# Opening of an attention and MLP kernel: second half of the first batch beside the first-pass steps, and constant products on TensorE

## The chip, the cores and the metric

The kernel runs on one core of one Trainium2 chip. Times are device microseconds (us) of one execution. A profiled execution has a span, from its first to its last instruction, and its own time, which also holds what lies around the span.

## The reference

The input is x of 4 batches x 1024 tokens x 256 channels. Two sandwich layers follow.

```python
x = x + layernorm(attention(layernorm(x)))
x = x + layernorm(ffn(layernorm(x)))
```

Attention has 16 heads of 16 channels. Its weights are binarized: each of Wq, Wk, Wv, Wp is replaced by its sign times the mean of its magnitudes, and each product adds a bias. Scores are scaled by 1/4 and go through softmax. The MLP has ternary weights: `silu(x w1 s1) * (x w2 s2)`, then two hidden layers of 1024 with exact gelu, then a product back to 256 channels.

## The kernel before

**What TensorE multiplies.** Products are done in fp32r, one pass. To keep fp32 accuracy a value is split into a high and a low fp32r piece, and both are multiplied; weights that are signs or ternary need no low piece. Where a product has plain fp32 operands (the means L249, L996, L1003, the bias L405, the last projection L1407), the trace shows two rows for each instruction.

**The opening** (from L193, before the branch) is one list of instructions for each engine. x of batch 0 comes in two halves of 512 tokens. VectorE (DVE) measures the first half (`measure_half(0)`: `bn_stats` and `bn_aggr` on four tiles, then `rstd` on GpSimd, POOL). ScalarE (ACT) takes magnitudes and signs of the four weights. TensorE (PE) sums the magnitudes of Wq and Wk into `al` (L249) and the flag `fl` (L259), from which every engine later decides a branch: the fast path if no weight is over 2 (L1441). DVE normalizes the first half (`xn_first`), measures the second half (`measure_half(1)`), TensorE transposes the first half (L284), and ACT and DVE write the high and low pieces (L286, L287).

**The attention** starts behind the branch, again in an order written out by the program. Work is counted in steps. A block is one group of 4 heads and 512 queries and has 8 steps; there are 4 batches x 4 groups x 2 = 32 blocks. The first pass (L722) multiplies queries by keys, and DVE takes the maximum of each 128x512 tile (L731): four tiles in each step. The second pass (L768) multiplies keys by queries with the maxima subtracted by a third product, ACT takes the exponential (L778), and `attend` (L794) multiplies it by the values. The first pass runs ahead: it starts at step `first` = -10, the second pass at step 0. So in the ten steps from -10 to -1 TensorE has first-pass products and jobs, and no second pass.

`slots(s)` gives the products of step s in five parts, and jobs are put in two places of a step: `run_jobs(s, 0)` after the third part, `run_jobs(s, 1)` after the last. `place((s, slot), job)` chooses the place. Tiles of `through` (seven PSUM banks) are chosen by `bank()` from planned times of PE, ACT and DVE; each engine works off its list in order.

Ahead of step -10 TensorE has in the fast path: the two `first_heads` jobs for the first half of queries and keys (L566; ACT scales and adds the bias twice, L572 and L579, and DVE makes the low piece of q or the mixed piece of k, L584 and L587), and the two `turn` jobs (L477) that transpose the second half, which DVE has normalized (`norm(1, nc.vector)`, L465). The jobs in the ten steps are: `first_heads` for the second half, four `value` jobs (L494), four parts of the next group's queries and keys (L535, whose pieces POOL splits, L548 and L549), the two means `alphas` (L996, L1003), `projection_bias` (L405) and the transposition of the maxima (`shift`, L748).

**The MLP** (`mlp`) works on 8 blocks of 512 tokens. `gated` makes h; `hidden` twice makes g1 and g2 with eight chunks of 128 hidden channels each; `done(c)` of a chunk runs gelu on ACT (L1261), the split on DVE (L1188, L1189), and then whatever jobs `beside` holds for that chunk. In block 0 these are `norm` and `turn` of block 1 and the last eighth of attention's projection: `scale_y` (L1394) and `last_projection` (L1407, L1412, L1413), which multiplies, adds the bias, and normalizes into x.

Of the kernel before, what the change touches and what calls it, by code (L numbers as in the profile page):

```python
# [40 lines left out]
P = 128  # L41
# [5 lines left out]
def sandwich_kernel(  # L47
# [157 lines left out]
    with ExitStack() as octx:  # L205
# [17 lines left out]
        nc.vector.tensor_scalar(turned, lower, -2.0, 1.0, ALU.mult, ALU.add)  # L223
        first_stats = []

        def measure_half(i):
            mv = moments(NT // 2, f"x0_{i}")
            for n in range(NT // 2):
                measure_one(mv, n, x_sb[:, 0, i * NT // 2 + n, :], f"x0_{i}")
            first_stats.append((mv, rstd(mv[:, :, 1], NT // 2, f"x0_{i}")))  # L230

        measure_half(0)
        most = small.tile([P, 4], F32, tag="most", name="most", bufs=1)
# [12 lines left out]
        for i, n in enumerate("qk"):  # L246
            for c in range(KC + 1):
                for k in range(KC):
                    nc.tensor.matmul(  # L249
                        al[:, c, i : i + 1],  # L250
                        mag_of[n][:, k, bass.ts(c, P)] if c < KC else mag4[n][:, k, :],
                        avg[:, 0:1], start=(k == 0), stop=(k == KC - 1),
                    )
# [5 lines left out]
        nc.tensor.matmul(fl, large, row_ones, start=True, stop=True)  # L259

# [19 lines left out]
        measure_half(1)  # L280
        tr = [ps_p.tile([P, 512], F32, tag=f"tr{k}", name=f"tr_first_{k}") for k in range(KC)]
        for k in range(KC):
            for i in range(NT // 2):
                nc.tensor.transpose(tr[k][:, bass.ts(i, P)], xn[:, i, bass.ts(k, P)], ident)  # L284
            hi, lo = (f[:, k, 0:512] for f in (xnT_sb, w1_sb))
            nc.scalar.copy(hi, tr[k])  # L286
            nc.vector.tensor_sub(lo, tr[k], hi.bitcast(F32))  # L287


    def attention(signs):  # L290


        with ExitStack() as actx:
# [267 lines left out]
            def first_heads(is_q, j):  # L561

                t = bank()
                for k in range(KC):
# [14 lines left out]
                got([t], "ACT", nc.scalar.activation(  # L579
                    full, through[:, t, :], AF.Identity, bias=bias4[:, n : n + 1],  # L580
                    scale=alpha4[:, n : n + 1],
                ))
# [402 lines left out]

            def run_jobs(s, slot):
                for job in jobs.pop((s, slot), ()):
                    job()

# [20 lines left out]
            if signs:  # L1010
                quadrants(0)
                norm(1, nc.vector)
                for is_q in (True, False):
                    first_heads(is_q, 0)
                for k in range(KC):
                    turn(1, k)

                place((first, 1), lambda: first_heads(False, 1))
                place((first + 1, 1), lambda: first_heads(True, 1))
                for i, n in enumerate("vp"):  # L1020
                    place((first + 6 + i, 0), lambda n=n: alphas(n))
                after = first + 2
            else:
                part = group_jobs(0)
                norm(0, nc.vector)
                for k in range(KC):
                    turn(0, k)
# [86 lines left out]
    def mlp(tag, low_too, wp):  # L1114
        with ExitStack() as fctx:
# [283 lines left out]
            def last_projection():  # L1399
# [3 lines left out]
                for m in range(2):  # L1403
                    zp = ps_o.tile([P, 512], F32, tag="o", name=f"zp{tag}_{m}")
                    for i in range(2):
                        for k in range(KC):
# [3 lines left out]
                            )  # L1410
                        z = zs[2 * m + i]
# [12 lines left out]
            for blk in range(blocks):  # L1424
# [4 lines left out]
                if blk == 0:  # L1429
                    beside[6] = [scale_y]  # L1430
                    beside2[5] = [last_projection]
# [66 lines left out]
```

## Time and profile before

| | |
|---|---|
| time, median of 3 runs | 1568.97 us (1566.95 to 1570.28) |
| profiled execution, own time | 1567.72 us |
| its span | 1565.9 us |
| busy in the span: PE, DVE, ACT, POOL | 98%, 69%, 53%, 28% |
| mean granted TensorE clock | 0.993 |
| first L722 product, first L768 product | 23.29 us, 55.48 us |
| last projection's products (L1407) | 970.35 to 976.6 us |

Busy time is what the rows of an engine cover. Rows of TensorE are pipelined and their ends are modelled, so that a busy TensorE is not at its peak; the time from one row's start to the next says more. In timeline rows the columns are start, time covered, engine, line, operation, tiles, shapes, and the number of instructions; in brackets stands the idle time before and what ended it. In a view by stretches each engine's busy time and number of rows is given, then the granted clock as a share of full speed, the DMA share and GB/s.

### The profile page before, as it was taken

To read this page: it belongs to the slowest core of one execution; us is meant where nothing else is said; L and a number is where in the kernel's file an instruction comes from. 1 tells how busy PE (TensorE), PEld (TensorE's weight loads), DVE (VectorE), ACT (ScalarE), POOL (GpSimd) and SP (SyncE) were. 2 spreads that over 40 slices of the span, in tenths; PEclk is the share of its full clock that TensorE was granted. 3 is DMA by queue.
4 is the path that set the end of the run, shared out by engine and by line. 5 is a ranking of instruction groups with operands and counts; after the bars stand their busy time and mean duration, and the time that the engine had idled before them with its cause. 6 is when DMAs were issued, how large, how long until landed. Compare 5 with 4: busy or idle time off the path is not lost.

```text
span 1565.9 us, 31822 instructions
## 1 busy us (share of the span) xinstructions
PE 1531.1 (98%) x12988; PEld 980.3 (63%) x12988; DVE 1075.2 (69%) x1960; ACT 829.2 (53%) x1496; POOL 437.4 (28%) x595
## 2 busy tenths in 40 slices
PE   7999999999999999999999999999999999999998
PEld 5544445444444444454444477888888888888887
DVE  6889887899787798878899554554545544455453
ACT  4577777677777677777777841413232313232321
POOL 2223143564424563314612150120202020202010
PEclk8999999999999999999999999999999999999999
DMA  1311521133132033311312040000000000000000
GB/s 58 72 30 33 144 49 29 24 72 74 39 76 59 22 65 72 66 30 31 75 36 73 8 139 0 1 14 1 14 1 14 1 14 1 14 1 14 1 14 17
DMA packets 35084, 58.55 MB, mean 37 GB/s; under 512 B 9968, under 2 KB 21488, under 8 KB 34928
## 3 DMA queue, kind: packets, MB, share of 16 engines
q1 hardware_dynamic: 29760, 43.57, 12.8%
q0 software_dynamic: 3792, 11.54, 2.3%
q8 instruction: 104, 1.70, 0.4%
q10 hardware_dynamic: 1376, 1.31, 0.2%
q14 instruction: 52, 0.43, 0.1%
HBM read 24.40 MB, written 4.19 MB: 18 GB/s over the span
## 4 chain that ended last, share of the span: by engine, by line
PE 85%; DVE 9%; ACT 4%; issue 1%; POOL 1%; DMA 1%; SPq 0%; DVEq 0%; ACTq 0%; POOLq 0%
PE g L1218 30%; PE y L794 14%; PE through L768 12%; PE through L722 10%; PE p L1218 7%; DVE nm L731 5%; PE fzp L1332 4%; PE through L535 2%; ACT e L778 2%; PE through L494 1%; PE through L748 1%; PE through L637 1%; ACT ys L809 1%; DVE bnstp_x L175 1%; DVE yt L835 1%
## 5 line engine op out<-in xcount | busy, mean ns | idle before, releaser
L731 DVE TENSOR_REDUCE nm<-through 128x1 f32<-128x512 f32 x1024 | 643.5, 680 | 115.6 <-PE through L722 59.3
L778 ACT ACTIVATE e<-through 128x512 f32<-128x512 f32 x1024 | 545.4, 603 | 160.7 <-PE through L768 141.7
L722 PE MATMUL through<-ks,qs 32*128 32x512 f32 x2048 | 462.2, 445 | 3.8 <-DVE nm L731 2.7
L768 PE MATMUL through<-qs,ks 32*128 32x512 f32 x2048 | 442.6, 434 | 11.1 <-ACT e L778 7.3
L768 PE MATMUL through<-nmT,ones_r 32*128 32x512 f32 x1024 | 348.7, 450 | 0.4 <-ACT nmT L755 0.4
L794 PE MATMUL y<-e,v 128*32 128x256 f32 x4096 | 323.0, 393 | 0.0
L722 PEld LDWEIGHTS through<-ks,qs 32*128 32x128 f32 x2048 | 215.7, 184 | 106.4 <-issue 82.5
L1218 PE MATMUL g<-g,h_sb 128*128 128x512 f32 x1024 | 235.7, 390 | 0.0
L768 PEld LDWEIGHTS through<-qs,ks 32*128 32x128 f32 x2048 | 201.8, 183 | 44.6 <-ACT e L778 20.5
L1218 PEld LDWEIGHTS g<-g,h_sb 128*128 128x128 f32 x1024 | 191.7, 188 | 39.5
L768 PEld LDWEIGHTS through<-nmT,ones_r 32*128 32x128 f32 x1024 | 137.6, 182 | 91.7 <-issue 88.7
L794 PEld LDWEIGHTS y<-e,v 128*32 128x32 f32 x4096 | 86.5, 108 | 170.8 <-issue 150.7
L1261 ACT ACTIVATE g2f<-g,sh_sb 128x512 f32<-128x512 f32 x64 | 44.1, 688 | 200.5 <-PE g L1218 180.8
L1261 ACT ACTIVATE g1f<-g,sh_sb 128x512 f32<-128x512 f32 x64 | 44.1, 689 | 170.1 <-PE g L1218 166.9
L164 POOL TENSOR_SCALAR ve_fz<-mvp_fz 128x4 f32<-128x4 f32 (+1 forms) x8 | 1.9, 232 | 468.5 <-DVE mvp_fz L176 468.5
L1218 PE MATMUL g<-h,h1b_sb 128*128 128x512 f32 x512 | 126.4, 389 | 0.0
L1218 PE MATMUL g<-h,h1a_sb 128*128 128x512 f32 x512 | 126.4, 389 | 0.0
L1188 DVE CAST g<-g2f 128x512 fp32r<-128x512 f32 x64 | 27.8, 434 | 142.0 <-ACT g2f L1261 142.0
L1218 PE MATMUL p<-xnT_sb,w_sb 128*128 128x512 f32 x512 | 117.7, 390 | 0.0
L1218 PEld LDWEIGHTS g<-h,h1a_sb 128*128 128x128 f32 x512 | 96.1, 188 | 19.9
L1218 PEld LDWEIGHTS g<-h,h1b_sb 128*128 128x128 f32 x512 | 96.1, 188 | 19.9
L1218 PEld LDWEIGHTS p<-xnT_sb,w_sb 128*128 128x128 f32 x512 | 95.6, 188 | 19.9 <-issue 0.4
(204 smaller groups left out, 1515.8 us busy)
## 6 DMA issues: line engine op xcount, KB each, us to landing
qs<-h1b_sb SPq DMA_DIRECT2D x240, 64.0 KB, 2.4
ks<-h1b_sb SPq DMA_DIRECT2D x120, 64.0 KB, 2.4
wraw<-in_dram SPq DMA_DIRECT2D x28, 256.0 KB, 2.7
h_sb<-in_dram POOLq DMA_DIRECT2D x4, 1024.0 KB, 8.5
yT<-yt SPq DMA_DIRECT2D x112, 32.0 KB, 2.0
out_dram<-x_sb SPq DMA_DIRECT2D x7, 512.0 KB, 2.8
x_sb<-in_dram SPq DMA_DIRECT2D x3, 1024.0 KB, 5.3
w_sb<-in_dram POOLq DMA_DIRECT2D x3, 1024.0 KB, 8.4
```

Source lines behind the costliest of these rows:

```text
L175: nc.vector.bn_stats(st, z)
L494: put(t, nc.tensor.matmul(through[:, t, bass.ts(i, C)], xnT_of[b][j][:, k, bass.ts(2 * m + i, P)], w_in["v"][:, k, :], start=(k == 0 and j ...
L535: put(t, nc.tensor.matmul(through[:, t, :], w_in[tag][:, k, bass.ts(c, P)], xnT_of[b][i][:, k, bass.ts(j, 512)], start=(k == 0 and i == 0) ...
L722: put(t, nc.tensor.matmul(through[:, t, :], q_of[u][n][rows, bass.ts(qt, P)], k_of[u][rows, bass.ts(j, 512)], start=(n == 0), stop=(n == 1),))
L731: got([t], "DVE", nc.vector.tensor_reduce(nm_of[blk][:, n4, j, g : g + 1], through[:, t, :], AX.X, ALU.max, negate=True))
L768: t, nc.tensor.matmul(through[:, t, :], lhs, rhs, start=(n == 0), stop=(n == 2)),
L778: exps.append(got([t], "ACT", nc.scalar.activation(e_of[s, g], through[:, t, :], AF.Exp)))
L794: nc.tensor.matmul(y_of[blk][32 * g : 32 * g + 32, cols], v_sb[n // 2][:, n % 2, :, :].rearrange("p h d -> p (h d)")[:, bass.ds((4 * g4 + ...
L1188: nc.vector.tensor_copy(hi, full)
L1218: nc.tensor.matmul(out[c], wk, src[j][:, k, :], start=(k == 0 and i == 0 and j == 0), stop=(k == n_k - 1 and i == len(ws) - 1 and j == 1),)
L1261: nc.scalar.activation(g, ps, AF.Gelu, scale=scale[:, c : c + 1])
L1332: nc.tensor.matmul(out_ps[i][:, :C], g2[j][:, k, bass.ts(i, P)], wk, start=(k == 0 and n == 0 and j == 0), stop=(k == NF - 1 and n == len( ...
```

## The change

1. Ahead of the branch 60 products of the constant `avg` with itself (plain fp32, 128x128, into a PSUM tile `hot` that nobody reads) are put into TensorE's list: 28 ahead of the means, 8 after each of the first two groups of means, 2 after each of the small ones, 8 after the flag, and 4 after the transposes. The means are reordered: the full ones of q and k, then the small ones.
2. Of the second half's four tiles DVE measures two before and two after the low pieces of the first half.
3. In the attention, for steps below 0, each `run_jobs` also issues 4 products of `ones_r` with itself (fp32r, 128x128), so 80 in all.
4. The second half is normalized on POOL instead of DVE, and its `turn` jobs move from before the first pass to slot 1 of the second step and slot 0 of the third. `first_heads` of the second half move from the first two steps to the fourth; `value` jobs start two steps later; the means `alphas` move to the sixth and eighth step.
5. In `first_heads` of the first half, the second scaling is made on DVE instead of ACT.
6. In the MLP's block 0, `scale_y` and `last_projection` move from chunk 6 of g1 and chunk 5 of g2 to chunks 0 and 2 of g1, `norm` of block 1 from chunk 2 to chunk 6 of g1; and all four products of a bank of `zp` come before DVE reads it.

```diff
+        hot = ps_p.tile([P, P], F32, tag="hot", name="hot")
+
+        def keep_going(n):
+            for _ in range(n):
+                nc.tensor.matmul(hot, avg, avg, start=True, stop=True)
+
...
-        def measure_half(i):
-            mv = moments(NT // 2, f"x0_{i}")
-            for n in range(NT // 2):
+        def measure_half(i, tiles=range(NT // 2)):
+            if 0 in tiles:
+                first_stats.append([moments(NT // 2, f"x0_{i}")])
+            mv = first_stats[i][0]
+            for n in tiles:
...
         measure_half(0)
+        keep_going(28)
...
+        for cs, behind in ((range(KC), 8), ([KC], 2)):
+            for i, n in enumerate("qk"):
+                for c in cs:
+                    for k in range(KC):
...
+                keep_going(behind)
...
         nc.tensor.matmul(fl, large, row_ones, start=True, stop=True)
+        keep_going(8)
...
-        measure_half(1)
+        measure_half(1, range(2))
...
             nc.vector.tensor_sub(lo, tr[k], hi.bitcast(F32))
+        keep_going(4)
+        measure_half(1, range(2, NT // 2))
...
-                got([t], "ACT", nc.scalar.activation(
-                    full, through[:, t, :], AF.Identity, bias=bias4[:, n : n + 1],
-                    scale=alpha4[:, n : n + 1],
-                ))
+                if j == 0:
+                    got([t], "DVE", nc.vector.tensor_scalar(
+                        full, through[:, t, :], alpha4[:, n : n + 1], bias4[:, n : n + 1],
+                        ALU.mult, ALU.add,
+                    ))
+                else:
...
+            hot = ps.tile([P, 512], F32, tag="y", name="hot")
+
             def run_jobs(s, slot):
                 for job in jobs.pop((s, slot), ()):
                     job()
+                if signs and s < 0:
+                    for _ in range(4):
+                        nc.tensor.matmul(hot[:, :P], ones_r, ones_r, start=True, stop=True)
...
-                norm(1, nc.vector)
+                norm(1, nc.gpsimd)
                 for is_q in (True, False):
                     first_heads(is_q, 0)
-                for k in range(KC):
-                    turn(1, k)
-
-                place((first, 1), lambda: first_heads(False, 1))
-                place((first + 1, 1), lambda: first_heads(True, 1))
+
+                place((first + 1, 1), lambda: turn(1, 0))
+                place((first + 2, 0), lambda: turn(1, 1))
+                place((first + 3, 0), lambda: first_heads(False, 1))
+                place((first + 3, 1), lambda: first_heads(True, 1))
                 for i, n in enumerate("vp"):
-                    place((first + 6 + i, 0), lambda n=n: alphas(n))
-                after = first + 2
+                    place((first + 5 + 2 * i, 1), lambda n=n: alphas(n))
+                after = first + 4
...
                                 wp[:, k, :].bitcast(F32), start=(k == 0), stop=(k == KC - 1),
                             )
+                    for i in range(2):
                         z = zs[2 * m + i]
...
                 if blk == 0:
-                    beside[6] = [scale_y]
-                    beside2[5] = [last_projection]
+                    beside = {0: [scale_y], 2: [last_projection], 6: beside[2]}
```

More of the change, by code (lines that the diff above doesn't have):

```diff
@@ L223, in sandwich_kernel @@
         nc.vector.tensor_scalar(turned, lower, -2.0, 1.0, ALU.mult, ALU.add)
+        hot = ps_p.tile([P, P], F32, tag="hot", name="hot")
+        def keep_going(n):
+            for _ in range(n):
+                nc.tensor.matmul(hot, avg, avg, start=True, stop=True)
         first_stats = []
-        def measure_half(i):
-            mv = moments(NT // 2, f"x0_{i}")
-            for n in range(NT // 2):
+        def measure_half(i, tiles=range(NT // 2)):
[3 more added lines that the diff above has]
+            for n in tiles:
                 measure_one(mv, n, x_sb[:, 0, i * NT // 2 + n, :], f"x0_{i}")
-            first_stats.append((mv, rstd(mv[:, :, 1], NT // 2, f"x0_{i}")))
+            if NT // 2 - 1 in tiles:
+                first_stats[i].append(rstd(mv[:, :, 1], NT // 2, f"x0_{i}"))
         measure_half(0)
+        keep_going(28)
         most = small.tile([P, 4], F32, tag="most", name="most", bufs=1)
@@ L245, in sandwich_kernel @@
         al = ps_p.tile([P, 3, 2], F32, tag="al", name="al")
-        for i, n in enumerate("qk"):
-            for c in range(KC + 1):
-                for k in range(KC):
[L249 to L253, printed above, removed]
+        for cs, behind in ((range(KC), 8), ([KC], 2)):
+            for i, n in enumerate("qk"):
+                for c in cs:
+                    for k in range(KC):
+                        nc.tensor.matmul(
+                            al[:, c, i : i + 1],
+                            mag_of[n][:, k, bass.ts(c, P)] if c < KC else mag4[n][:, k, :],
+                            avg[:, 0:1], start=(k == 0), stop=(k == KC - 1),
+                        )
+                keep_going(behind)
         large = small.tile([P, 1], F32, tag="largep", name="large", bufs=1)
@@ L578, in first_heads @@
                 n = 1 - is_q
-                got([t], "ACT", nc.scalar.activation(
-                    full, through[:, t, :], AF.Identity, bias=bias4[:, n : n + 1],
-                    scale=alpha4[:, n : n + 1],
-                ))
+                if j == 0:
[4 more added lines that the diff above has]
+                else:
+                    got([t], "ACT", nc.scalar.activation(
+                        full, through[:, t, :], AF.Identity, bias=bias4[:, n : n + 1],
+                        scale=alpha4[:, n : n + 1],
+                    ))
                 if is_q:
@@ L1011, in attention @@
                 quadrants(0)
-                norm(1, nc.vector)
+                norm(1, nc.gpsimd)
                 for is_q in (True, False):
                     first_heads(is_q, 0)
-                for k in range(KC):
-                    turn(1, k)
-                place((first, 1), lambda: first_heads(False, 1))
-                place((first + 1, 1), lambda: first_heads(True, 1))
+                place((first + 1, 1), lambda: turn(1, 0))
+                place((first + 2, 0), lambda: turn(1, 1))
+                place((first + 3, 0), lambda: first_heads(False, 1))
+                place((first + 3, 1), lambda: first_heads(True, 1))
                 for i, n in enumerate("vp"):
-                    place((first + 6 + i, 0), lambda n=n: alphas(n))
-                after = first + 2
+                    place((first + 5 + 2 * i, 1), lambda n=n: alphas(n))
+                after = first + 4
             else:
```

## The prediction

> **What bounds the kernel now.** I read the chain that ended last first: TensorE (PE) holds 85% of it, so a delay of TensorE anywhere in the opening passes through the attention loop to the end. The chain inside the first 56 us is carried by TensorE blocks:
>
> ```profile
> 9.69 3.57 PE al L249 x16
> 17.02 2.06 PE through L566 x4
> ...
> 29.48 1.68 PE through L494 x8
> ...
> 42.91 1.15 PE through L494 x8
> ```
>
> The same eight products of L494 take 1.68 us at 29.5 and 1.15 us at 42.9. The view by stretches says why:
>
> ```profile
> 24.49:29.84 5.35, 4.50 (x22) 2.55 (x23) 3.63 (x7) 3.11 (x4) 0.00 (x0) 1.00 0.00 2
> 29.84:40.08 10.24, 10.24 (x42) 6.99 (x41) 6.46 (x12) 1.95 (x3) 1.89 (x2) 0.50 0.01 2
> 40.08:55.48 15.40, 15.39 (x90) 9.12 (x90) 13.66 (x23) 5.00 (x9) 6.35 (x11) 1.00 0.05 9
> ```
>
> After the length the columns are PE, weight load, DVE, ACT, POOL, then the granted clock. It is 0.50 from 29.84 to 40.08. That is what the products in the ten steps are aimed at. Before 23 us the column reads 1.00, but the rows don't: eight 512-column products of L566 start 0.43 us apart from 17.02 to 20.57, and 0.24 apart at 24.5. So the front also runs at half rate.
>
> Is TensorE idle in the steps, so that added products are free? The timeline at full clock, where the time from one block's start to the next is what a block costs:
>
> ```profile
> 42.17 0.73 PE L722 MATMUL through<-ks,qs 32*128 32x512 f32 x3
> 42.84 0.39 PE L494 MATMUL through<-w_sb,xnT_sb 128*128 128x256 f32 x1
> ...
> 43.98 0.75 PE L722 MATMUL through<-ks,qs 32*128 32x512 f32 x8
> 44.66 1.05 PE L996 MATMUL through<-avg,yT_last 128*128 128x1 f32 x8
> 45.65 0.73 PE L722 MATMUL through<-ks,qs 32*128 32x512 f32 x5
> 46.31 0.50 PE L535 MATMUL through<-xnT_sb,w_sb 128*128 128x512 f32 x1
> ...
> 47.44 0.73 PE L722 MATMUL through<-ks,qs 32*128 32x512 f32 x3
> 48.10 1.13 PE L1003 MATMUL through<-yT_last,avg 128*128 128x256 f32 x4
> 49.16 1.26 PE L722 MATMUL through<-ks,qs 32*128 32x512 f32 x8
> ```
>
> A block of first-pass products costs 0.66 us whether it holds 3 or 5, and 0.68 with 8. L494 costs 1.15, L535 and L566 1.13, L996 0.99, L1003 and L405 1.06, four transposes (L748, 54.14 to 54.73) 0.59. The blocks stand end to end. DVE needs 4 x 0.60 = 2.4 us of maxima a step, TensorE about 3.4. TensorE is the bound there, clock or not.
>
> **Part by part.**
>
> *The first pass, before.* From 23.29 to 55.48 (the first L768) are 32.2 us. Blocks in order: 15 of L722 (10.0), two of L566 (2.3), four of L494 (4.6), four of L535 (4.5), L996, L1003, L405, L748 (3.7): 25.1 us at full clock. The rest is 4.4 lost to the half clock (the seven blocks from 29.41 to 40.38 took 11.0 and cost 6.6 at full clock) and 2.7 of waits.
>
> *The first pass, after.* Twenty groups of four products of ones_r come in, one in each half step; the first falls into idle time before the first pass, 19 lie inside. Each also cuts a run of eight first-pass products into two blocks: 19 blocks instead of 15 (12.5, and 0.35 for the last one). The jobs are the same (15.1), and two turns of 0.59 move in (1.2). No row shows a 128x128 fp32r product. Its weight load is 128 columns wide as in L996, whose eight rows start 0.114 apart; streaming 256 columns (L494) goes at 0.12. I take 4 x 0.112 plus the change of kind (L996 has about 0.1 over its rows): 0.57 a group, 10.8 in all. Bounds: 0.35 (the four stream at half of L494's rate and reload nothing) and 1.0 (0.22 each, what 128 columns in plain fp32 would take by L1003's rows): 6.7 to 19. Sum 39.9 us.
>
> To this come two waits. The second half's normalization goes to POOL: L465 takes 1.22 us there (24 rows) against about 0.4 on DVE, behind the 2.7 us of constants that POOL writes from 17.11 to 19.80. With the front below, its four tiles are ready at about 31.9; TensorE stands at the first turn from 30.0 on, and all first-pass blocks queue behind it: 1.5 us. The next L535 waits 0.4 for the low half of the second turn. So 41.8 instead of 32.2: +9.6. The 2.7 us of former waits go; DVE, with 36 maxima and 3 us of other work (24.5), fits under it.
>
> *The clock.* TensorE will have nothing from about 24 to 26.9 (last L566 product to first first-pass product) and little at the turn. In before a stretch of 3.4 us with PE busy for 0.75 of it (26.4 to 29.84, and again 733.0 to 736.4) was followed by half clock, for 10.2 us here and for 3.4 us there. So I expect the products not to prevent one drop around 27 to 30. A stretch costs at most 1.7 us; I take two, 3.4 (bounds 0 and, with the clock low for all the first pass, 39.9 x 4.4/6.6 = 27).
>
> The Trainium skill, "TensorE: Matmul & The Clock Gate", section on HAM oscillation, names idle gaps over about 3.4 us as what brings the half rate (its next section lets short idle times do so too, without a measure). Here it came with no idle gap over 1.2 us, so the trace does not bear the rule out; by it the 3.4 would drop out (1581.3). The same page, Back-to-back issue gap, gives about 81 ns for a sustained 128-column product; the nearest row has 112, and by the page the 19 groups would be an estimated 2.4 us cheaper. Neither changes the sign.
>
> *Ahead of the branch.* 56 products of avg stand before the first transpose. Each is plain fp32, two rows: at half rate 0.43 (L249: 12 rows in 2.70, 0.213 apart), at full rate 0.223 (L996's spacing; half of L1003's for the streaming). The front of before:
>
> ```profile
> 10.56 2.70 PE L249 MATMUL al<-avg,mag_k 128*128 128x1 f32 x12
> 13.19 0.19 PE L259 MATMUL fl<-row_ones,large 128*1 128x1 f32 x2
> 13.31 1.97 PE L284 MATMUL tr_first<-ident,xn_first 128*128 128x128 f32 x8
> 17.02 0.77 PE L566 MATMUL through<-xnT_sb,w_sb 128*128 128x512 f32 x1 [1.74 <-DVE w_sb L287]
> ```
>
> The clock rose at 23.0, 6.0 us after dense work began at 17.0, so I let it rise 6.0 us after 1.1: 14 products cold and 14 warm end at 10.2. The means (24 rows, 2.7), fl (0.1) and 28 more products (6.2) put the first transpose at 19.3 instead of 13.31. That is a queue on TensorE: everything behind waits. Then the warm clock gives back: transposes, copies and DVE's subtractions end at 21.95 (16.87 before), since only two of the four measures stand ahead of the subtractions; L566's blocks take half as long, and with `full` on DVE (0.62 behind ACT's 0.78) ks is ready at 26.85 instead of 23.24. +3.6 us (bounds +1.0, all warm, and +7).
>
> *The tail of attention's projection in the MLP.*
>
> ```profile
> 970.35 1.02 PE L1407 MATMUL zp<-wp_sb,yT_last 128*128 128x256 f32 x4
> 972.86 1.99 PE L1407 MATMUL zp<-wp_sb,yT_last 128*128 128x256 f32 x8 [1.49 <-DVE z L1412]
> 975.44 1.13 PE L1407 MATMUL zp<-wp_sb,yT_last 128*128 128x256 f32 x4 [0.59 <-DVE z L1412]
> ```
>
> TensorE waits for DVE's read of the half bank: 5.9 us for 16 rows that need 3.6. With all four products of a bank ahead of DVE both waits go, -2.2. In the new place TensorE arrives at 929.56, when chunk 2 is done; DVE has then chunk 0's split (until 929.95) and the scaling (2 x 0.48, L1394) before it: 1.3 us of a new wait. Net -0.9 (0 to -2.2). The normalization of block 1, now in chunk 6, has twenty us until its turn: nothing.
>
> **Sum.** +3.6 +9.6 +3.4 -0.9 = +15.7 on the span of 1565.9. The profiled run's own time is 1567.72, so 1583.4; the median is 1.25 above it: 1584.7.
>
> **Rivals.**
>
> *Cheap products* (1572 to 1577): groups at 0.35, no drop, warm from the start: +1.0 +9.6 -4.1 -2 gives +4.5. For it: nothing shows this product. Against: a load precedes every product in each row.
>
> *The clock stays low through the opening* (1590 to 1608): in before three stretches with PE busy at 1.00 did not raise it, and the new steps hold less streaming. The full 27 instead of 3.4 gives 1608. Against: at 517.9 and 736.4 it was back after one stretch.
>
> *Faster* (1565.5): the products find free slots, the clock holds, and the first pass runs at DVE's pace. First maximum at 27.95, 24.5 us of DVE: the first L768 at 52.9 instead of 55.5, and -0.9 later. It decides where a half step leaves TensorE 0.57 us of slack; in 42.17 to 49.16 I find none, and 49.16 to 50.35 (1.19 for a 0.68 block) is the only place where it waited for DVE. That the products fail to hold the clock at all is inside the second rival.
>
> **How the numbers follow.** About 0.2% (3.1 us) can be told from no change. The forecast, +8 to +21 (1577 to 1590), 0.60; cheap products 0.13; clock low 0.14; no change 0.04; faster 0.09. The range of 1572 to 1604 leaves out the last two and the end of the third. Slower 0.87.
>
> **What would show it.** Right: first transpose near 19, first pass beginning near 27, groups of four on the new line costing about 0.57 from start to start, the first L768 (its new line) near 69 to 72, a clock of 0.50 for some stretch between 26 and 36, TensorE waiting on POOL at the first turn, no wait inside zp but one before it. Wrong: the first second-pass product before 57, or groups whose removal of idle time shows as DVE without gaps in the ten steps.

## The result, and the profile after

The kernel after takes 1605.91 us (median of 4 runs, 1599.3 to 1608.15), the kernel before 1568.48 beside it (1566.95 to 1570.28). The ratio is 1.0248, with an interval of 1.0217 to 1.0279: slower by 37 us. The profiled execution took 1608.15 us with a span of 1606.3, against 1567.72 and 1565.9 before, so the two traces differ by 40.4 us. A run more than 1.5% above the fastest of its kernel counts as slow and stands outside the ratios given here; there is one, of 1600.88 us in experiment 2.

First the row of the page that gives the granted clock in 40 slices of 40 us, then the view by stretches, with the columns of before (time and rows of PE, weight load, DVE, ACT, POOL; granted clock; DMA):

```profile
PEclk8569999999999999999999999999999999999999
```

```profile
5.79:26.28 20.49, 17.52 (x146) 16.71 (x145) 12.04 (x33) 7.58 (x17) 7.96 (x28) 1.00 0.18 56
26.28:60.00 33.72, 33.08 (x118) 23.96 (x119) 16.12 (x25) 6.47 (x10) 9.36 (x10) 0.50 0.01 3
60.00:104.78 44.78, 44.53 (x204) 31.07 (x203) 19.08 (x31) 10.79 (x20) 5.79 (x9) 0.50 0.20 35
104.78:150.00 45.22, 44.89 (x528) 21.17 (x528) 36.35 (x60) 32.87 (x63) 9.31 (x15) 1.00 0.12 34
```

The front runs at full clock from 5.79 on, as it was meant to. Then the clock falls at 26.28 and stays at 0.50 for 78.5 us, through the whole first pass and into the second. In all that time TensorE is shown busy for 77.6 of 78.5 us. Busy did not bring the clock back.

The timeline (start, time covered, engine, line, tiles, shapes, number; in brackets the idle time before and what ended it) shows where it fell and what a block costs afterwards:

```profile
18.89 1.04 PE L298 MATMUL tr_first<-ident,xn_first 128*128 128x128 f32 x8
...
23.51 0.56 PE L1016 MATMUL hot<-ones_r 128*128 128x128 f32 x4
```

```profile
26.93 1.22 PE L744 MATMUL through<-ks,qs 32*128 32x512 f32 x5 [2.85 <-DVE ks L609]
28.08 1.11 PE L1016 MATMUL hot<-ones_r 128*128 128x128 f32 x4
29.12 1.22 PE L744 MATMUL through<-ks,qs 32*128 32x512 f32 x3
...
32.47 1.11 PE L493 MATMUL through<-ident,xn 128*128 128x128 f32 x4
...
40.22 0.95 PE L1016 MATMUL hot<-ones_r 128*128 128x128 f32 x4
41.09 1.22 PE L744 MATMUL through<-ks,qs 32*128 32x512 f32 x3
...
93.03 0.80 PE L790 MATMUL through<-qs,ks 32*128 32x512 f32 x2
...
100.88 1.94 PE L816 MATMUL y<-e,v 128*32 128x256 f32 x16
```

First transpose at 18.89, first pass at 26.93 after 2.85 us without a product. From then on blocks are slow: a first-pass block (L744) goes 1.15 us from start to start instead of 0.66, a group of four 0.87 (40.22 to 41.09, after a job) to 1.04 (28.08 to 29.12). The first second-pass product (L790) stands at 93.03; the corresponding L768 of before stood at 55.48. That is 37.6 of the 40.4 us, and all of it is there before step 0.

In the MLP the edit did its work. All 16 rows of the last projection follow each other, with one wait ahead of them:

```profile
972.27 3.72 PE L1435 MATMUL zp<-wp_sb,yT_last 128*128 128x256 f32 x16 [0.97 <-DVE yT_last L1422]
```

**Which share of the array is used.** PE's busy time does not tell why the clock stayed down, so I worked out another number from the rows. A dense row of 512 columns starts 0.427 us after the one before at half clock, and I take half of that at full clock; columns in proportion; a plain fp32 row counts twice where the profile shows it once (transposes and products of `avg`). Each product counts by the part of the 128x128 array it covers, so a first-pass product (32 rows) counts a quarter. Weight loads count nothing. The sum over a stretch of 3.413 us (the length of the single dips, and every change of the clock here falls on that grid), divided by the stretch, is the share. It is an estimate: whether a row's columns are counted from its start or spread over the row moves a share by up to 0.06. In the kernel before the clock fell after a stretch with a share of 0.34 (26.43 to 29.84), stayed low through 0.72 and 0.67 and came back after 0.82. In the kernel after it fell after 0.24 (22.86 to 26.28), and the stretches that followed in the first pass had 0.22 to 0.71, none more. The theory that the experiments are to test: **the clock goes by the streamed share, with two thresholds far apart; the new groups and the moved jobs hold the share in the gap between them, so one fall lasts to the end of the first pass.**

### The profile page after: what moved, and what is told of

It is laid out like the page before. It is cut to its first block, busy times and chain, and to the rows that moved or that the text cites. A ratio compares the mean times of both kernels' runs of the same rounds, so it can differ in the third digit from the quotient of the medians.

```text
span 1606.3 us, 32219 instructions
## 1 busy us (share of the span) xinstructions
PE 1578.6 (98%) x13188; PEld 1022.1 (64%) x13188; DVE 1074.2 (67%) x1958; ACT 828.0 (52%) x1494; POOL 442.6 (28%) x599
## 4 chain that ended last, share of the span: by engine, by line
PE 86%; DVE 8%; ACT 3%; issue 1%; POOL 1%; DMA 0%; SPq 0%; DVEq 0%; ACTq 0%; POOLq 0%
PE g L1246 29%; PE y L816 14%; PE through L790 12%; PE through L744 10%; PE p L1246 7%; DVE nm L753 5%; PE fzp L1360 4%; PE through L551 2%; ACT e L800 2%; PE through L510 1%; PE through L770 1%; PE hot L229 1%; PE hot L1016 1%; PE through L659 1%; ACT ys L831 1%
## 5 line engine op out<-in xcount | busy, mean ns | idle before, releaser
L744 PE MATMUL through<-ks,qs 32*128 32x512 f32 x2048 | 473.9, 456 | 5.6 <-DVE ks L609 2.9
L790 PE MATMUL through<-qs,ks 32*128 32x512 f32 x2048 | 445.2, 436 | 11.3 <-ACT e L800 7.6
L790 PE MATMUL through<-nmT,ones_r 32*128 32x512 f32 x1024 | 350.9, 453 | 0.4 <-ACT nmT L777 0.4
L744 PEld LDWEIGHTS through<-ks,qs 32*128 32x128 f32 x2048 | 220.7, 189 | 105.2 <-issue 80.2
L790 PEld LDWEIGHTS through<-qs,ks 32*128 32x128 f32 x2048 | 203.8, 184 | 44.7 <-ACT e L800 21.5
L790 PEld LDWEIGHTS through<-nmT,ones_r 32*128 32x128 f32 x1024 | 138.7, 183 | 92.2 <-issue 89.1
```

What stands on the lines that cost most here:

```text
L744: put(t, nc.tensor.matmul(through[:, t, :], q_of[u][n][rows, bass.ts(qt, P)], k_of[u][rows, bass.ts(j, 512)], start=(n == 0), stop=(n == 1),))
L790: t, nc.tensor.matmul(through[:, t, :], lhs, rhs, start=(n == 0), stop=(n == 2)),
```

## The experiments

Times here are medians beside runs of the kernel before on the same chip; the kernel after did not run beside them, so a difference from its 1605.91 us is good to a few us only. The runs of before scatter more than in the first comparison (1560.4 to 1574.4 over three sets), and so do some variants, because the stretches run on freely and a fall comes or not by where they lie. Over 48 runs of before, a line through time against time at half clock (twice one minus the mean granted clock, times the run's time) has 0.37 us lost per us at half clock, and 1559.0 at none; I use such lines below to take the clock out.

**1. The change without the groups of four.** Against the kernel after:

```diff
-                if signs and s < 0:
-                    for _ in range(4):
-                        nc.tensor.matmul(hot[:, :P], ones_r, ones_r, start=True, stop=True)
```

> The changed kernel without the 80 products of ones_r in the ten steps; all else stays, the 60 products of avg ahead of the branch too. Theory (the clock falls in the idle time before the first pass, 24.1 to 26.9 us, and comes back only after a stretch of 3.4 us in which the array is used for about three quarters; the groups of four small products hold TensorE for 0.87 us and use the array for 0.43 of it, so they keep the steps under that): the clock falls near 26 as in the changed kernel, but the steps are as dense as those of before, and it returns after 3 to 6 stretches; first second-pass product near 62, time 1573 to 1579. Rival A (the moved jobs make the steps thin, the products have no part in it): the clock stays at 0.50 until about 75 or later, time 1583 or more. Rival B (the clock is a side matter, the 80 products' own time on TensorE is the loss): about 1570, whatever the clock does.

Measured 1590.62 us (1589.07 to 1591.92), ratio 1.0169 (1.0136 to 1.0202). The clock is at 0.50 from 26.3 to 87.7. So the groups of four are not what keeps the clock down; my theory's number was missed and the first rival's held. The first pass with its jobs moved later (highest share of a stretch before the second pass 0.73) does not bring the clock back by itself either.

**2. The groups of four alone.** Against the kernel before: the same lines added to `run_jobs`.

> The kernel before with nothing added but the 80 products of ones_r in the ten steps. Theory: in before, the stretch from 26.4 to 29.8 uses the array for about a third and the clock falls after it; two groups add 0.12, so it holds or nearly holds. If it holds, the products cost their own time: 19 groups of 0.57 and four cut blocks, some 14 us, less the 4.4 of low clock: 1577 to 1581, first second-pass product near 65. If it falls all the same, it stays low for most of the first pass, as in the changed kernel: 1588 to 1600. Rival A (products of constants do not count for the clock at all): it falls at about 30 as in before and stays low: 1588 or more. Rival B (own time alone): 1582 with the same 10 us of low clock as in before.

Measured 1584.2 us (1569.39 to 1600.88, 10 runs), ratio 1.0087 (1.0053 to 1.012), on three levels: three runs at 1569.4 to 1570.8 with a mean clock of 0.998 or more, six at 1582 to 1586 with 0.986 to 0.988, one at 1600.9 with 0.975. The line through the nine runs of the first two levels has 0.39 us per us at half clock and 1568.3 at none. So the groups cost 9.3 us with the clock held (the expectation had some 14), and up to 17 more by the clock in these nine. In the profiled run (1585.48) the clock fell at 46.80. The stretches around it, and the rows:

```profile
22.91:43.39 20.48, 19.89 (x127) 14.65 (x127) 15.17 (x25) 6.86 (x10) 3.02 (x4) 1.00 0.01 1
43.39:46.80 3.41, 3.41 (x27) 2.54 (x26) 2.26 (x5) 0.59 (x1) 0.76 (x1) 1.00 0.23 38
46.80:80.93 34.13, 33.88 (x157) 23.12 (x156) 16.03 (x26) 8.48 (x16) 5.78 (x9) 0.50 0.22 40
```

```profile
43.35 0.56 PE L993 MATMUL hot<-ones_r 128*128 128x128 f32 x4
43.84 0.73 PE L722 MATMUL through<-ks,qs 32*128 32x512 f32 x5
44.51 0.66 PE L993 MATMUL hot<-ones_r 128*128 128x128 f32 x4
45.10 0.73 PE L722 MATMUL through<-ks,qs 32*128 32x512 f32 x3
45.76 1.05 PE L1001 MATMUL through<-avg,yT_last 128*128 128x1 f32 x8
46.67 1.00 PE L993 MATMUL hot<-ones_r 128*128 128x128 f32 x4
47.60 1.22 PE L722 MATMUL through<-ks,qs 32*128 32x512 f32 x5
```

This stretch is the plainest evidence of the whole case: in the stretch ahead of the fall TensorE is busy 3.41 of 3.41 us, the blocks stand end to end, and the clock falls. What fills the stretch is first-pass blocks on a quarter of the array, groups of four, and L1001 (the means `alphas`), eight rows of one column in 0.91 us. Its share is 0.26.

**3. A bridge over the idle time.** Against the kernel after:

```diff
                 if signs and s < 0:
-                    for _ in range(4):
+                    early = s < first + 3
+                    for _ in range(12 if (s, slot) == (first, 0) else 3 if early else 0):
+                        nc.tensor.matmul(hot, ones_r, xnT_sb[:, 0, 0:512], start=True, stop=True)
+                    for _ in range(0 if early else 4):
                         nc.tensor.matmul(hot[:, :P], ones_r, ones_r, start=True, stop=True)
```

> The changed kernel with the idle time before the first pass filled: twelve 512-column products of ones_r and the first high piece in the first slot of step -10, and three of them instead of the four small ones in each other half step up to step -8; from step -7 on the four small ones as in the changed kernel. Theory: TensorE's clock holds at full through the first pass, since it never has a stretch under a third; a group of four small ones costs about 0.57, first second-pass product at 68 to 73, time 1580 to 1586. Rival A (moved jobs or constant products cannot hold the clock): it falls once the wide products end, near 40, and the time is 1593 or more. Rival B: as the changed kernel, about 1605.

Measured 1576.56 us (1574.42 to 1591.59, 5 runs), ratio 1.0095 (1.0046 to 1.0144): three runs at 1574.4 to 1576.6 with a clock of 0.997 to 0.999, two at 1590.2 and 1591.6 with 0.986 and 0.987. The theory had 1580 to 1586. Filling the gap ahead of the first pass (27 wide products in place of 24 of the small ones) took away 29 us. In the profiled run the clock held until 51.24 and fell after the stretch with `alphas` in it (share 0.39), as in the run before.

**4. One wide product in place of each group of four.** Against the kernel after:

```diff
-                    for _ in range(4):
-                        nc.tensor.matmul(hot[:, :P], ones_r, ones_r, start=True, stop=True)
+                    nc.tensor.matmul(hot, ones_r, xnT_sb[:, 0, 0:512], start=True, stop=True)
```

> The changed kernel with each group of four 128-column products replaced by one 512-column product of ones_r and the first high piece: the same 512 columns streamed with one weight load. Theory: the clock falls near 26 as in the changed kernel, but a group now takes about 0.55 instead of 0.87 at half clock for the same use of the array, the steps reach three quarters, and the clock returns within 3 to 7 stretches (36 to 50 us); first second-pass product at 70 to 80, time 1580 to 1592. Rival A (these steps cannot raise the clock): low until the second pass has begun, about 1599. Rival B (own time alone): 19 x 0.3 less than the changed kernel, about 1600.

Measured 1579.05 us (1574.24 to 1580.02), ratio 1.0094 (1.0062 to 1.0126), a little under the expected range. The profiled run fell at 25.46 like the kernel after, but was back at 39.11, after a stretch with a share of 0.75 (the three stretches before it, of 0.32 to 0.68, had not brought it back). From start to start such a product costs 0.32 us after a job where the four cost 0.49. The wide product also streams x where the four stream ones; constant operands alone are not what fails, though: in the kernel after, the products of `avg` at the front brought the clock to full at 5.80.

**5. Wide or streaming nothing, at the same price in time.** Two variants of the kernel before whose groups take TensorE about as long as the four, with opposite shares. One has two products of `avg` with one column:

```diff
+                if signs and s < 0:
+                    for _ in range(2):
+                        nc.tensor.matmul(hot[:, :1], avg, avg[:, :1], start=True, stop=True)
```

> The kernel before with, in each half step of the first ten steps, two products of avg with a single column of avg (four rows, about 0.45 to 0.6 us of TensorE as a group of four costs, but next to nothing streamed) in place of the change's groups of four. Theory: what the clock goes by is how much of the array's time is streamed in a stretch of 3.4 us; these groups take the same time from TensorE and stream nothing, so the share falls below 0.35 early in the first pass and never comes to 0.75: half clock from about 27 to 33 until the y products of the first query group, the first second-pass product at 85 to 97, 1592 to 1612 in every run. Rival: the clock goes by TensorE's busy time, weight loads among it, and falls only in idle time: as with the groups of four alone, 1569 to 1586.

and the other two of 512 columns:

```diff
+                if signs and s < 0:
+                    for _ in range(2):
+                        nc.tensor.matmul(hot, ones_r, xnT_sb[:, 0, 0:512], start=True, stop=True)
```

> The kernel before with, in each half step of the first ten steps, two products of 512 columns (0.47 us at full clock, nearly all of it streamed) in place of the change's groups of four, which take 0.49 after a job. Theory: the same time from TensorE, but the share of the array in use stays above 0.4 in every stretch of the first pass, that with the products of alphas among them: the clock holds from 23 us on in all or nearly all runs, first second-pass product at 62 to 65, 1568 to 1572, and none of the spread to 1585 that the groups of four alone gave. Rival: the fall at the alphas comes from something else (a phase, chance): the same two levels, 1570 and 1585, about as often as with the groups of four alone.

One column: 1599.0 us (1598.24 to 1600.98, all five runs), ratio 1.0229 (1.0216 to 1.0242). 512 columns: 1572.5 us (1570.93 to 1584.13, 6 runs), ratio 1.0057 (1.0044 to 1.007); five runs at 1570.9 to 1574.8, one fell at 47.80 after the stretch with `alphas` (share 0.37). TensorE is shown busy almost without a break in both; the clock tells them apart. First the one-column variant's first pass by stretches, then the first pass of the 512-column one up to its fall:

```profile
25.28:59.42 34.14, 34.14 (x130) 26.04 (x129) 13.86 (x23) 7.00 (x10) 3.77 (x4) 0.50 0.03 5
```

```profile
20.50:44.39 23.89, 22.18 (x120) 13.95 (x118) 16.49 (x27) 9.50 (x15) 3.28 (x4) 1.00 0.00 1
44.39:47.80 3.41, 3.41 (x21) 2.00 (x20) 2.32 (x4) 0.57 (x2) 0.52 (x1) 1.00 0.23 38
```

In the first row PE is busy for 34.14 of 34.14 us at a clock of 0.50 throughout. Busy time, weight loads included, as what raises the clock is excluded by this row. For the wide pairs I had expected none of the spread to 1585; one run in six still fell.

**6. The front and the moved jobs.** First the kernel after without its front products (`keep_going` and its calls are taken out, which is all 60 products, the 4 after the first transposes among them), then without any constant product (also the lines of experiment 1):

> The kernel after without its 56 products of avg in the front; the groups of four in the ten steps, the moved jobs and the edit in the MLP stay. Theory: the front term (+3.6 us for the first pass) is real, and the clock falls in the idle time that the front leaves ahead of the first pass. Without the 56 products the first transpose stands near 13.3 again and ks is ready at 22 to 24 instead of 26.9; the clock rises near 23 as in the kernel before, and what follows depends on where the stretches of 3.4 us fall: 1570 where the clock holds, 1580 to 1600 where it falls. Rival: the groups of four and the moved jobs keep the clock down by themselves whatever the front does: 1598 to 1606 in every run, and half clock through the whole first pass.

> The kernel after without any of the constant products (neither the 56 in the front nor the groups of four): what is left is the moved jobs, the normalization on POOL, one subtraction pair of the measures later, and the edit in the MLP. Theory: at half clock L572 streams only 3.5 us without a break (15.48 to 19.0 in the run without the front products), as the turn's transposes no longer follow it, so hardly ever does a stretch of 3.4 us lie wholly inside; the clock does not rise there, and the rest of the first pass has no dense stretch either: ks at about 21.8, half clock until the first y products near 80, 1580 to 1590 in most runs, and 1558 to 1566 in a run where it does rise. Rival: without the groups the moved jobs are harmless, as dense as in the kernel before: 1558 to 1568 in all runs, half clock over by 24 to 40.

Without the front products: 1599.35 us (1598.17 to 1600.93), ratio 1.0224 (1.0211 to 1.0237), the rival's number. ks was ready at 21.8, so the front term is real (26.93 with them), but the time is hardly better. The rows:

```profile
16.48 0.63 PE L572 MATMUL through<-xnT_sb,w_sb 128*128 128x512 f32 x1
16.90 0.63 PE L572 MATMUL through<-w_sb 128*128 128x512 f32 x1
...
21.80 1.22 PE L734 MATMUL through<-ks,qs 32*128 32x512 f32 x5 [1.81 <-DVE ks L599]
```

512 columns go every 0.43 us, a first-pass block takes 1.15: the whole opening runs at half clock from the start. (The granted clock of this run reads 1.00 before 553 us and 0.997 in the mean; the record lacks the opening, and the rows decide.) In the kernel before these eight products were followed at once by eight transposes, 5.5 us without a break, and the clock rose at 23. The change moved the transposes into the first pass; what is left is 3.6 us of L572 and one group of four, and the best stretch there has a share of 0.68.

Without any constant product: 1582.86 us (1582.3 to 1583.24), ratio 1.0107 (1.0072 to 1.0142), as expected, with this detail against the expectation: in the profiled run the stretch from 15.51 to 18.92 did raise the clock (share 0.90), and the next, with 2.56 us of waiting for ks, took it away again until 73.5. So the moved jobs, even with the edit in the MLP, cost 15.5 us, although the first pass began at 21.48 instead of 23.29: the clock stood at 0.50 from 22.34 to 73.53.

**7. The edit in the MLP alone.** Against the kernel before:

```diff
-                    beside[6] = [scale_y]
-                    beside2[5] = [last_projection]
+                    beside = {0: [scale_y], 2: [last_projection], 6: beside[2]}
...
+                    for i in range(2):
                         z = zs[2 * m + i]
```

> The kernel before with only the edit in the MLP (all four products of a bank ahead of VectorE's reads, the scaling and the projection's tail in earlier chunks). Theory: -0.9 to -1.4 us on the span, both old waits inside zp gone and one new wait of about 1 us ahead of it: runs of 1559 to 1568, a median 1 to 2 below the kernel before. Rival: the waits only change place, no difference to 0.3 us.

Measured 1563.1 us (1559.26 to 1566.79, 12 runs), ratio 0.9987 (0.9973 to 1.0001). The sign is as expected; the interval includes no difference. The traces say more: from the 3585th of the 4096 `y` products to the end of the span are 750.8 us in before (1565.9 less 815.1) and 749.5 here (1560.2 less 810.7), 749.6 in the kernel after. The edit is worth 1.3 to 1.4 us.

**8. Out of the trap.** Against the kernel after, twenty wide products once, after the clock has fallen:

```diff
+                    for _ in range(20 if (s, slot) == (first + 1, 0) else 0):
+                        nc.tensor.matmul(hot, ones_r, xnT_sb[:, 0, 0:512], start=True, stop=True)
```

> The kernel after with twenty products of 512 columns added in the first half of the second step, after the clock has fallen. Theory: the half clock is a trap with one way out, a stretch of 3.4 us with the array nearly full; the twenty give two such stretches (8.5 us at half clock), the clock returns at 33 to 38 and then stays as long as no stretch falls below about 0.35: half clock for 7 to 12 us instead of 78, first second-pass product at 73 to 80 instead of 93, 1587 to 1594 although more work was added; up to 1604 where it falls again at the alphas. Rival: the clock is set by what the steps are, not by how they are entered (it falls again at once): 1610 to 1616.

Measured 1595.34 us (1593.89 to 1599.09), ratio 1.0195 (1.0159 to 1.0231): 10 us faster than the kernel after, with more work in it. That is a little over the 1587 to 1594 of the theory, and within its second case, up to 1604 where the clock falls again at the alphas. The view by stretches shows both:

```profile
22.95:26.36 3.41, 1.14 (x8) 0.88 (x6) 2.46 (x4) 1.56 (x2) 3.38 (x13) 1.00 0.00 0
26.36:33.19 6.83, 6.21 (x19) 4.21 (x20) 3.14 (x5) 0.00 (x0) 5.57 (x6) 0.50 0.00 0
33.19:53.67 20.48, 19.98 (x123) 15.12 (x121) 12.51 (x20) 6.57 (x10) 3.32 (x4) 1.00 0.01 1
53.67:57.08 3.41, 3.41 (x25) 2.54 (x25) 1.87 (x3) 0.61 (x2) 0.47 (x1) 1.00 0.22 38
57.08:91.22 34.14, 33.89 (x147) 24.85 (x145) 15.46 (x26) 8.41 (x15) 5.79 (x9) 0.50 0.19 34
```

Idle time takes the clock (share 0.22). The dense stretch from 29.78 to 33.19 (0.82) gives it back. The steps keep it for 24 us. The busy stretch with `alphas` (0.28) takes it again, and the steps, the same in kind, do not get it back for 34 us. The rival, that the clock falls again at once, is excluded by the 24 us.

**9. The change with the clock held.** Against the kernel after, the bridge, and pairs of wide products instead of the groups:

```diff
-                    for _ in range(4):
-                        nc.tensor.matmul(hot[:, :P], ones_r, ones_r, start=True, stop=True)
+                    for _ in range(12 if (s, slot) == (first, 0) else 2):
+                        nc.tensor.matmul(hot, ones_r, xnT_sb[:, 0, 0:512], start=True, stop=True)
```

> The kernel after with twelve products of 512 columns ahead of the first pass (in the idle time from 24 to 27 us) and two of them in place of each later group of four. Theory: only the clock made the change cost 37 us; with it held, what is left is the front (3.6 to 4.1), the pairs (19 of 0.47 to 0.6: about 9 to 11) and -1.4 in the MLP, over the 1560.5 of the kernel before with the clock held: 1571 to 1576 in most runs, and about 1585 to 1590 in those where the stretch with the alphas falls. Rival: the moved jobs and POOL's normalization cost by themselves as well: 1580 or more even where the granted clock is 0.997 and more.

Measured 1579.45 us (1578.09 to 1581.39), ratio 1.0083 (1.0057 to 1.0109), between the two numbers. All runs lost some clock (0.995 or 0.996), so the rival's condition did not come about. By the 0.39 us per us of experiment 2 the 13 to 16 us at half clock in their mean clocks would be 5 to 6 us, which leaves an estimated 1573 to 1574, in the range of the theory; no run shows it. The rows of the profiled run show what took the clock:

```profile
30.74 0.80 PE L493 MATMUL through<-ident,xn 128*128 128x128 f32 x3
32.41 0.33 PE L493 MATMUL through<-ident,xn 128*128 128x128 f32 x1 [0.87 <-POOL xn L481]
...
34.28 1.20 PE L1016 MATMUL hot<-xnT_sb,ones_r 128*128 128x512 f32 x2
```

With TensorE at full clock it reaches the turn before POOL has normalized the last tile, and waits 0.87 us. The stretch around it (30.72 to 34.13) has a share of 0.37, and the clock falls there, until a stretch of 0.78 ends it at 44.37.

**10. A version that beats both.** Against the kernel before: the edit in the MLP, and nine wide products where TensorE waited in the first two steps:

```diff
+                if signs and s < 0:
+                    for _ in range({(first, 0): 3, (first, 1): 2, (first + 1, 1): 4}.get((s, slot), 0)):
+                        nc.tensor.matmul(hot, ones_r, xnT_sb[:, 0, 0:512], start=True, stop=True)
```

> The kernel before with the edit in the MLP and nine products of 512 columns in the three places of the first two steps where TensorE waited (three ahead of the first pass, two in its first step, four in its second). Theory: about 2 us of TensorE, 1.2 to 1.8 of them in idle time; the stretches between 22 and 30 us stay over 0.4 in use, so the fall at 25 to 30 us is gone: 1558 to 1562 in nearly all runs, against 1561 to 1570 of the kernel before. Rival: the fall comes later in the first pass instead, or the products cost their full 2 us on top: 1562 to 1570, no difference from the edit in the MLP alone.

Measured 1561.99 us (1559.07 to 1564.38, 12 runs) against 1567.36, ratio 0.997 (0.9953 to 0.9988): faster, by about 5 us, of which the edit in the MLP is 1.3 to 1.4. Six of the twelve runs lie above the 1562 under which nearly all were expected. In the profiled run the clock holds from 21.21 to 55.34, and is then at 0.50 until 62.17, as in that of the edit in the MLP alone (56.08 to 62.91); the stretch from 24.62 to 28.04 has a share of 0.79, where the kernel before had 0.34 a little later. The four products of the second step lie in the former wait:

```profile
27.44 0.40 PE L566 MATMUL through<-w_sb 128*128 128x512 f32 x1
27.68 1.08 PE L993 MATMUL hot<-xnT_sb,ones_r 128*128 128x512 f32 x4
28.69 0.73 PE L722 MATMUL through<-ks,qs 32*128 32x512 f32 x3
```

The three L722 start at 28.69; in before the last two of them started at 28.76, after 0.84 us of waiting for DVE. So these four cost nothing. Runs of the edit in the MLP alone lie between 1559.3 and 1566.8, of this version between 1559.1 and 1564.4: what the nine products take away may be the upper end. The two were not run side by side, so this is not shown.

**The shares together**, all by the estimate above, as far as step -1:

| | share of the stretch (kernel, its start) |
|---|---|
| clock fell after it | 0.24 (after, 22.86); 0.34 (before, 26.43); 0.26 (groups alone, 43.39); 0.37 (wide pairs, 44.39); 0.39 (bridge, 47.82); 0.35 (one wide, 22.05); 0.22 and 0.28 (burst); 0.37 (experiment 9, 30.72); 0.16 to 0.32 (experiments 1, 5, 7 and without products, their first falls) |
| stayed at full clock | 0.37 (one wide, 49.35); 0.42 (bridge, 30.76); 0.43 (groups alone, 22.91); 0.44 (before, 43.49) and more |
| stayed at half clock | up to 0.71 (after), 0.72 (before, bridge, without front products), 0.73 (experiment 1, and without products) |
| clock rose after it | 0.75 (one wide, 35.70); 0.77 (MLP alone, 25.36); 0.78 (experiment 9); 0.82 (before, 36.67; burst); 1.00 (after, 2.38) |

Falling below about 0.38, rising above about 0.74, keeping what it is in between: within the error of the estimate all rows of the first pass fit. The values on the two sides of each bound lie closer together than that error, so the bounds are known to some 0.05. From step 0 on neither bound fits. At the start of the `y` products (100.88 in after) the clock came back after a stretch that I put at 0.55, and the single dips at 517.9 and 736.4 in before ended after one stretch of that kind. Products on quarters of the array (128*32, four side by side) run there, and it may be that they count for more than their part. Over all traces the rises from step 0 on come after 0.49 to 0.73, and one stretch of 0.75 (wide pairs, 75.11) was followed by none; the falls come after 0.32 to 0.37, but some 40 stretches of the attention loop with 0.29 to 0.36 were followed by no fall. With products of 128*32 counted in full these rises come after 0.72 and more, but some falls of the attention loop then come after 0.42 to 0.51 instead of 0.32 to 0.37, and stretches of up to 0.86 stay at half clock. No run was aimed at this; it stays open.

## Why the prediction was wrong

The forecast was 1584.7 (1572 to 1604) with 0.87 on slower. Slower it is, but 1605.9 lies beyond the range. By its own steps, against the span's difference of 40.4 us:

- **The front, +3.6**: right. First transpose 18.89 (19.3 forecast), ks and the first pass at 26.93 (26.9), the warm-up products ending at about 9.7 instead of 10.2.
- **The groups**: 0.57 us forecast at full clock. In the run of the groups alone they cost 0.49 after a job (43.35 to 43.84) and 0.59 after a first-pass block (44.51 to 45.10). With the blocks that they cut in two, by the line through nine runs, 9.3 us, against 10.9 by the working (38.7 without the turns, less 27.8 of before without its clock loss). 1.6 us too dear. The bounds held.
- **The wait for POOL, 1.5**: not there in the kernel after. Its tile was due at 31.9 as worked out, but TensorE at half clock came to the turn only at 32.47. With the clock nearly held it is 0.87 us (experiment 9). The step was right for the clock it assumed, and it mattered more as a sparse stretch than as a wait.
- **The clock, +3.4**: this is the step that failed: how long the clock stays low. The fall itself was forecast, with its cause (nothing to do from 24 to 26.9) and its place; the length was taken as two stretches and was 23. Against the 41.8 and 3.4 us forecast between the first L744 and the first L790, the trace has 66.1: 20.9 us too little at this one place, and 1.5 and 2.5 more to the first `y` products and over the attention loop.
- **The MLP, -0.9**: 1.3 to 1.4 gained. Both waits inside `zp` went, and the new one was 0.97 instead of 1.3.

Sorted by work and clock, the account closes to about 1 us. Work at full clock: the front 3.6, the groups 9.3, the two turns that now lie in the first pass 0.8 (0.41 and 0.42 in the burst's trace; 0.59 each forecast), POOL 0.9, MLP -1.3, so 13.3. Clock: within their spans the traces have 88.4 us at 0.50 after and 20.6 before; 68 us more at 0.39 us per us (the line of the groups alone, the nearest in kind) make 26. Together 39, of 40.4 measured. The terms come from different kernels, so this is a check and no proof of each one. The prediction had about 16.7 for the work and, since it let the 4.4 us of before's clock loss go, -1.0 for the clock.

**Why the length was misjudged.** The rival *the clock stays low through the opening* had the right reason, that three stretches with PE busy at 1.00 did not raise the clock in before and that the new steps stream less, and about the right price (1608 for all of it, where the median is 1605.91 and the profiled run took 1608.15). That the price comes so near is in part luck: it holds 1.9 us of waits that were not there in the kernel after and groups 1.6 us too dear, and leaves out the 4.0 us behind the first L790. It got 0.14 for the argument that at 517.9 and 736.4 the clock was back after one stretch. Those dips lie in the attention loop, where other products run. The nearest rows were those of the first pass itself, 29.84 to 40.08, and there it took a share of 0.82 to come back, in a stretch holding parts of two `value` jobs. The new order has no such stretch. I counted how long TensorE would be busy and what a stretch costs; how much it would stream in each stretch, which could be added up from the same rows, I left out. The range also ended at 1604 because only the beginning of that rival was taken into it.

**What decides against the change** is then, in the order of size: the clock (26 of 40 us), which it loses at the idle gap ahead of the first pass that the moved transposes leave (2.85 us, and 2.56 without any constant product); the 80 products in steps that have no room for them (9.3); the 60 products ahead of everything (3.6). Taking out any one part leaves most of the clock's loss in place (experiments 1 and 6), since what is left without any constant product already ends at 1582.9.

## What to carry to other kernels

Constant products paid here only where they streamed columns and fell into idle time: put 512-column products into the waits, not small ones between blocks that already stand end to end. Before costing a clock dip, add up the streamed share per stretch of 3.4 us over the new order and see whether any later stretch is dense enough to end it; if none is, a single gap of 3 us can put the whole stage at half clock, as it did here. And compare several runs: where a stage lives between the thresholds, one kernel has levels 15 us apart.

## What the runs showed of the hardware

- The clock fell with TensorE busy in 3.41 of 3.41 us (experiment 2), and stayed at 0.50 with TensorE busy in 34.14 of 34.14 (experiment 5, one column). The Trainium skill, "TensorE: Matmul & The Clock Gate", Part 1 on the clock gate, gives half clock after a window of some 3.4 us idle and full clock after one busy. The window's length agrees with every dip here (3.4 us or a multiple); idle and busy do not, unless, for the products of the first pass, busy means some three quarters of the array streamed and idle under about four tenths.
- Each us at half clock cost 0.37 (before) to 0.39 us (groups alone), not 0.5: blocks grow to less than twice their length, a first-pass block from 0.66 to 1.15 us, L551 from 1.13 to 1.88 (38.34 to 40.22 in the kernel after).
- Half clock in the records can be missing: in the run without front products the granted clock reads 1.00 over the whole opening, with 512 columns every 0.43 us. Its five runs have mean clocks of 0.974 to 0.999 and times within 3 us. Spacing of rows is the safer reading.
- A group of four 128x128 fp32r products costs 0.49 us, half as much again as the 0.32 of one 512-column product that streams the same columns.
